# A decoder layer on one core: the second group's first steps moved between the first group's, constants made before zero transfers, PSUM reads ranked first, list transfers yielded in pairs

## The chip, the cores and the metric

The kernel runs on one core of a Trainium2 chip. The metric is the device time of one execution in microseconds (us), lower is better; the median of three runs is given. Engines are named as in the profile: PE (TensorE: matmul, and PEld for its weight loads), DVE (VectorE), ACT (ScalarE), POOL (GpSimd) and SP (SyncE, here a queue that only issues transfers). PSUM is the memory of eight banks that PE writes its results to and DVE and ACT read from.

## What is computed

One decoder layer in f32 on x of 32 batches x 112 tokens x 256, with a context of 375 tokens per batch. Three sublayers, each after a layernorm and each added to x: a delta-rule attention with an MLP, cross attention with 16 heads of 16, and a mixture of 6 experts (two for each token) with one shared expert.

```python
def _L0_attn_ref(x, ...):
    h = _rmsnorm(x, norm1_w)
    q = h @ Wq
    k = h @ Wk
    k = k / jnp.maximum(jnp.linalg.norm(k, axis=-1, keepdims=True), 1e-12)
    v = _ema_scan(h @ Wv, jax.nn.sigmoid(alpha_logit))
    beta = jax.nn.sigmoid(h @ beta_w + beta_b)[..., 0]
    # S += beta_t (v_t - S k_t) k_t^T ;  o_t = S q_t
    attn_out = _delta_scan(q, k, v, beta)
    x = x + attn_out @ Wo
    h2 = _rmsnorm(x, norm2_w)
    return x + (jax.nn.silu(h2 @ w_gate) * (h2 @ w_up)) @ w_down

def _L0_xattn_ref(query, key, value, mask, ...):
    scores = jnp.einsum('bhqd,bhkd->bhqk', Q, K) / np.sqrt(hd)
    scores = jnp.where(mask[:, None, :, :] == 1, -1e9, scores)
    out = jnp.einsum('bhqk,bhkd->bhqd', softmax(scores), V)
    return out.transpose(0, 2, 1, 3).reshape(B, Sq, D) @ w_out.T

def _L0_ffn_ref(x, gate_w, gate_b, ...):
    probs = jax.nn.sigmoid(xt @ gate_w.T + gate_b)
    w, idx = jax.lax.top_k(probs, 2)
    w = w / (jnp.sum(w, axis=-1, keepdims=True) + 1e-08)
    # y = sum over the two experts of w * (silu(x ew1) * (x ew3)) ew2
    return y + (silu(xt @ fc1.T) * (xt @ fc2.T)) @ fc3.T

x = x + _L0_attn_ref(_layernorm(x), ...)
x = x + _L0_xattn_ref(_layernorm(x), ctx, ctx, mask, ...)
x = x + _L0_ffn_ref(_layernorm(x), ...)
```

## The kernel before

**Tiling.** The 32 batches are taken in 8 groups of GB = 4. A group's tile of x is 112 partitions (tokens) x 4 x 256.

**A planner sets the order.** The body doesn't issue instructions; it notes them in a `Recorder` (L76 to L359), which prices each and, in `flush` (L230), schedules them: of the instructions of an engine whose inputs are ready, it takes the one with the lowest `rank` (L227), which is the number of its place in the order of noting. The eight banks are handed out there too. PE, DVE and ACT then run their instructions in that fixed order; POOL's and SP's queues keep theirs, so a transfer that waits holds up those behind it. `flush` is called twice, at the start of the last group and at the end, so the schedule spans groups. All noted instructions have line L358 in the profile (those of the expert tiles L1306 and L1323), so the profile is read by the tiles' names. What stands ahead of the Recorder (L436 to L500: constants, zeroes) is issued directly.

**Generators.** Each piece of a group's work is a generator that yields after every step. `delta_block` (L676) is the first sublayer of a group: `layernorm` (L613) writes a and h, then beta (from hb, the product of h and nwb); `to_features` transposes h to hT and nT; Wk, Wq and Wv projections, the last with a scan (vE); then Gram products G and A, the triangular system W that goes through memory (`blocks`) into blocks L, is solved by DVE for group 0 and by POOL for the others, comes back as X and Y; levels of small products join the blocks (W, Y, X, C); then V, U, oT, x1, h2, and the MLP with gT. `queries` (L917) makes qz. In group 0 nothing else is there to run beside it but the keys and values (kx, vx) of the first batches, which L1429 deals out.

**The main loop** (L1446 to L1532) runs over 128 quads (batch, half and quarter of the heads), 16 per group: `scores` (L966), softmax on DVE and ACT (e, nmx), `turned` (L993, transposes into eT), `product` (L1005, eT by vx), `cross_out` (L1025). Between them it draws steps of three piles: `main`, the first sublayer of the next group (`ahead`), as many as keep its share of the priced work level; `others`, the expert sublayer of the group before (`mixture_sparse`: `route` L1046, `dispatch` L1079, `shared` L1128); and kv, the keys and values of the next batch.

**Experts.** Groups 0 to 6 send their tokens to experts through eight lists in memory: `dispatch` writes the places of the tokens by indirect transfers on POOL; `tables` (L1179) gathers the lists, and `sparse_tiles` runs 54 tiles of 128 tokens (L1306, L1323). The last group runs all experts densely. During the last group's quads `tiles` (tables and the sparse tiles) are drawn after a table of numbers (L1479).

**Buffers.** A `Ring` (L47) hands out buffers of a tag in turn; an instruction that writes a buffer waits for the last reader of what it held. Tag "a", "vo" and "qk" of the delta block have one buffer each, so a second group's a, vE or gT waits for the first group's to be read.

Of the kernel before, what the change touches and what calls it, by code (L numbers as in the profile page):

```python
# [70 lines left out]

class Node:
    __slots__ = ("at", "eng", "cost", "lag", "calls", "before", "after", "banks", "keys", "start", "end", "left", "seen")


class Recorder:  # L76
# [87 lines left out]
    def add(self, name, op, outs, ins, call, cost=None, loose=False):  # L164
# [8 lines left out]
        if not joins:  # L173
            node = Node()
            node.at, node.eng, node.cost, node.lag = len(self.nodes), eng, 0.0, 0.0
            node.calls, node.before, node.after, node.banks, node.keys = [], {}, [], [], set()
            node.start = node.end = None
            node.seen = own if self.whole is None else None
            self.nodes.append(node)
            if self.whole is not None:  # L180
                self.held, node.cost = node, self.whole
# [44 lines left out]

    def rank(self, node):  # L227
        return node.at
# [134 lines left out]
def tile_decoder(ctx: ExitStack, tc: tile.TileContext, t: dict, out: bass.AP):  # L363
# [28 lines left out]
    room = {"mk": SK, "e": 4 * SK, "eT": KC * 4 * T, "qz": 4 * NT, "x": GB * D, "neg": SK, "h": GB * D, "rs_i": 2 * GB, "rs_u": 2 * GB}  # L392
# [68 lines left out]
    for table in lists:  # L461
        nc.gpsimd.dma_start(out=table.rearrange("(p l) o -> p (l o)", p=TM), in_=zeros)
    nothing = moe.tile([P, t["fc3T"].shape[0] // P, NT], F32, tag="hT", name="nothing")
    nothing = nothing[:T].rearrange("p c n -> p (c n)")[:, : NB * FAR // T]
    nc.vector.memset(nothing, 0.0)
    for table in blocks[1:]:
        nc.gpsimd.dma_start(
            out=table.rearrange("n f -> (n f)").rearrange("(p q) -> p q", p=T), in_=nothing
        )
# [29 lines left out]
    for vx in vxs:  # L499
        nc.gpsimd.memset(vx[:, :, :, 1, :], 0.0)  # L500

# [111 lines left out]
    def layernorm(dst, src, rms=None):  # L613
# [15 lines left out]
        for b in range(GB):  # L629
            nc.vector.tensor_scalar(  # L630
                dst[:, b, :], src[:, b, :], mv[:, b, 0:1], r[:, b : b + 1], ALU.subtract, ALU.mult
            )
        if rms is not None:
            off = stat("off")
            nc.vector.scalar_tensor_tensor(off, mv[:, :, 0], -1.0, r[:, GB:], ALU.mult, ALU.mult)
            for b in range(GB):
                nc.scalar.activation(
                    rms[:, b, :], src[:, b, :], AF.Identity, bias=off[:, b : b + 1], scale=r[:, GB + b : GB + b + 1]
                )

# [35 lines left out]
    def delta_block(g, xt):  # L676

        a = dlt.tile([T, GB, D], F32, tag="a", name=f"a_{g}")
# [16 lines left out]
        vE = dlt.tile([P, NC, NT], F32, tag="vo", name=f"vE_{g}")  # L695
# [193 lines left out]
        gT = dlt.tile([P, HID // P, NT], F32, tag="qk", name=f"gT_{g}")  # L889
# [189 lines left out]
    def dispatch(g, a3, place, ge):  # L1079
# [27 lines left out]
        for b in range(GB):  # L1107
            for c in range(2):
                i = g * GB + b
                nc.gpsimd.indirect_dma_start(  # L1110
                    out=lists[2 * b + c][:], out_offset=bass.IndirectOffsetOnAxis(ap=row_i[:, c, i : i + 1], axis=0),
                    in_=number[:, c, i : i + 1], in_offset=None,
                )

# [13 lines left out]
    def shared(g, acc, aT, first=lambda: None):  # L1128
# [6 lines left out]
        for i, _ in enumerate(ffn(g, NE, aT, fc1, fc2, fc3, emit)):  # L1135
            yield
            if i == 0:
                first()
                yield
# [39 lines left out]
    def tables():  # L1179
# [52 lines left out]
        for i, table in enumerate(lists):  # L1232
# [7 lines left out]
            if i % GB == GB - 1:  # L1240
# [186 lines left out]

    early_kv = chained(keys_values(0), keys_values(1))
    for i, _ in enumerate(metered(ahead(0))):  # L1429
        for _ in range({5: 2, 6: 2, 7: 2, 8: 2, 9: 1, 11: 1, 18: 2}.get(i, 0)):  # L1430
            next(early_kv, None)
    drain(early_kv)
# [11 lines left out]
    main, others, out_of, kv = ahead(1), iter(()), iter(()), iter(())  # L1444
    at = 0
    for n in range(len(quads) + 2):  # L1446
# [29 lines left out]
        if last:  # L1476
            mains.append(main)
            side += [others] * ((0, 0, 0, 1, 1, 1, 2, 1, 1, 1, 1, 0, 0, 0, 0, 0)[i] if g < groups else 0)
            side += [tiles] * ((0, 0, 0, 0, 0, 0, 0, 1, 1, 1, 0, 1, 4, 4, 4, 4)[i] if g < groups else 3)  # L1479
        else:  # L1480
# [6 lines left out]
            whole = sum(costs) + (four_out + mixed if g else 0.75 * four_out)  # L1487
# [114 lines left out]
```

## Time and profile before

| | |
|---|---|
| median of three runs | 1462.86 us (1461.95 to 1462.88) |
| the profiled execution's own time | 1463.02 us |
| its span in the profile | 1461.2 us |
| PE busy | 1373.3 us (94%) |
| DVE, ACT, POOL busy | 967.8, 704.8, 319.8 us |
| mean clock granted to PE | 0.976 |

The profile shows one execution. The chain of work that ended last, followed back from the last instruction, is 79% PE, 11% DVE, 6% ACT, 3% issue and 1% POOL. An answer of the timeline gives the start, the length, the engine, the line, the operation and what it writes and reads; in brackets, how long the engine had stood idle and what ended that. A table of windows gives, for a stretch of time, the busy time of each engine and the clock. The stages, by the first and last instructions of each: group 0's first sublayer 0 to 130 us, the steady quads to 1132, the last group's quads with the lists to 1206, expert tiles to 1388, and the last group's dense experts and the stores to the end.

### The profile page before, as it was taken

What the parts mean: (1) busy time and instruction counts of PE and PEld (TensorE: products, weight loads), DVE (VectorE), ACT (ScalarE), POOL (GpSimd) and SP (SyncE); (2) the same over time, 40 slices, a digit from 0 to 9 for tenths busy, and PEclk for the clock granted to TensorE, in tenths of its full rate; (3) what the DMA queues carried; (4) which work ended last, traced back from release to release, by engine and by line L of the source; (5) the groups of instructions that cost most, each with busy time, mean ns of one, the idle gap of its engine ahead of it and who ended that gap; (6) DMA issues with size and microseconds to landing.
All of it is one profiled execution on the core that took longest, in us unless ns stands there. A gap on an engine that the chain in (4) does not pass through costs nothing.

```text
span 1461.2 us, 26685 instructions
## 1 busy us (share of the span) xinstructions
PE 1373.3 (94%) x9716; PEld 929.6 (64%) x9716; DVE 967.8 (66%) x3164; ACT 704.8 (48%) x1946; POOL 319.8 (22%) x492
## 2 busy tenths in 40 slices
PE   4479999999999999999999999999999879999998
PEld 2455766676667666766776677667766556666665
DVE  4547676775777578667866786678657645455577
ACT  2024756654665466546654665566546554322110
POOL 3010310320032003200320032003200324556400
PEclk9679999999999999999999999999999989999999
DMA  8100100101010101010101010101015111222283
GB/s 229 40 1 6 35 16 16 48 17 41 16 48 17 41 16 48 17 41 16 48 16 41 16 49 16 42 16 48 16 29 174 17 47 63 83 80 89 69 231 100
DMA packets 77170, 73.13 MB, mean 50 GB/s; under 512 B 29864, under 2 KB 72808, under 8 KB 77040
## 3 DMA queue, kind: packets, MB, share of 16 engines
q1 hardware_dynamic: 69296, 56.00, 14.0%
q0 software_dynamic: 7744, 15.43, 3.6%
q8 instruction: 77, 1.26, 0.4%
q14 instruction: 53, 0.43, 0.1%
HBM read 51.12 MB, written 20.28 MB: 49 GB/s over the span
## 4 chain that ended last, share of the span: by engine, by line
PE 79%; DVE 11%; ACT 6%; issue 3%; POOL 1%; DMA 0%; ACTq 0%; DVEq 0%; POOLq 0%
PE bank L358 69%; PE bank L1306 6%; PE bank L1323 3%; ACT e L358 3%; ACT h L358 2%; DVE rs_u L358 1%; DVE rs_i L358 1%; ACT eT L358 1%; DVE W L358 1%; DVE br L358 1%; DVE x L358 1%; DVE ms L358 1%; DVE vx L358 1%; DVE above L358 1%; POOL C L358 0%
## 5 line engine op out<-in xcount | busy, mean ns | idle before, releaser
L358 ACT ACTIVATE e<-e,nmx 112x375 f32<-112x375 f32 x512 | 306.2, 601 | 141.7 <-DVE nmx L358 141.4
L358 DVE CUSTOM_DVE_ANT_0 e<-bank,neg,flip 112x375 f32<-112x375 f32 x512 | 281.9, 604 | 47.9 <-PE bank L358 47.4
L358 ACT COPY eT<-bank 125x448 f32<-125x448 f32 x384 | 186.4, 531 | 165.6 <-PE bank L358 149.3
L358 PE MATMUL bank<-ident,e 112*125 112x112 f32 x1536 | 207.1, 279 | 12.3 <-DVE vx L358 6.6
L358 PEld LDWEIGHTS bank<-ident,e 112*125 112x125 f32 x1536 | 188.9, 190 | 46.1 <-issue 13.7
L358 PE MATMUL bank<-kx,qz 32*112 32x375 f32 x1024 | 126.2, 527 | 6.4 <-issue 4.4
L358 PE MATMUL bank<-eT,vx 125*32 125x112 f32 x3072 | 102.8, 264 | 5.0 <-issue 5.0
L358 PEld LDWEIGHTS bank<-eT,vx 125*32 125x32 f32 x3072 | 70.1, 109 | 57.2 <-issue 44.8
L1306 PE MATMUL bank<-ew,xT 128*128 x216 | 102.0, 595 | 1.8 <-ACT e L358 1.2
L358 PE MATMUL bank<-w_xwvT,cT 128*125 128x256 f32 x384 | 102.5, 393 | 0.5
L358 PE MATMUL bank<-cT,w_xwkT 128*128 128x375 f32 x256 | 100.1, 516 | 0.0
L358 DVE SCALAR_TENSOR_TENSOR hs<-hs,bank 128x256 f32<-128x256 f32 x108 | 45.4, 421 | 80.7 <-ACT hs L358 72.0
L358 ACT ACTIVATION_READ_ACCUMULATOR e<-e,nmx 112x1 f32 x512 | 97.2, 190 | 0.0
L358 POOL TENSOR_TENSOR u<-h,nwb 112x1024 f32<-112x1024 f32 x7 | 16.8, 2406 | 306.7 <-issue 306.7
L358 DVE SCALAR_TENSOR_TENSOR qk<-qk,bank 128x448 f32<-128x448 f32 x64 | 39.7, 621 | 64.5 <-ACT qk L358 35.6
L358 ACT ACTIVATE hs<-bank 128x256 f32<-128x256 f32 x54 | 20.7, 383 | 116.3 <-PE bank L1306 107.7
L358 PEld LDWEIGHTS bank<-w_xwvT,cT 128*125 128x125 f32 x384 | 66.6, 188 | 14.1 <-issue 4.1
L358 POOL DMA_INDIRECT lists<-number,row_i x56 | 53.0, 946 | 90.7 <-DVE tn L358 57.0
L358 PEld LDWEIGHTS bank<-cT,w_xwkT 128*128 128x128 f32 x256 | 46.0, 198 | 38.9 <-issue 10.2
L358 PEld LDWEIGHTS bank<-kx,qz 32*112 32x112 f32 x1024 | 42.8, 172 | 42.5 <-issue 18.7
L358 POOL DMA_INDIRECT xg<-rows,take x54 | 52.5, 972 | 71.9 <-PE bank L358 60.6
L358 PE MATMUL bank<-ident,h 112*128 112x112 f32 x256 | 40.9, 280 | 27.4 <-ACT h L358 25.2
(242 smaller groups left out, 2390.8 us busy)
## 6 DMA issues: line engine op xcount, KB each, us to landing
cT<-in_ctxT_dram SPq DMA_DIRECT2D x32, 375.0 KB
mk<-in_mask_dram SPq DMA_DIRECT2D x32, 164.1 KB
x<-in_x_dram SPq DMA_DIRECT2D x7, 448.0 KB
rows<-h SPq DMA_DIRECT2D x7, 448.0 KB
kept<-x SPq DMA_DIRECT2D x7, 448.0 KB
e<-results SPq DMA_DIRECT2D x6, 448.0 KB
eT<-results SPq DMA_DIRECT2D x4, 448.0 KB
out_dram<-x SPq DMA_DIRECT2D x4, 448.0 KB
```

The costliest lines, as they stand in the source:

```text
L358: getattr(getattr(self.nc, name), op)(*[real(a) for a in args], **{k: real(v) for k, v in kwargs.items()})
L1306: rec.nc.tensor.matmul(p.real(), xT[:, c, :], w13[:, bass.ds(at[i] * (NC * 2 * MI) + c * 2 * MI, 2 * MI)], start=(c == 0), stop=(c == NC - 1),
L1323: rec.nc.tensor.matmul(p[:, :D].real(), hT[:, c, :], w2[:, bass.ds(at[i] * (CH * D) + c * D, D)], start=(c == 0), stop=(c == CH - 1),)
```

## The change

1. **Own buffers for group 1.** A new `Ring.at` picks a buffer of a tag by number. Group 1's a takes the third buffer of x, its vE the second of "hT"; group 0's gT takes the second of "qz". So group 1 can start its first sublayer while group 0's is under way, and the load of x of group 2, which needs the third x buffer, waits for the reading of group 1's a.
2. **Group 1's first five steps** (layernorm and beta; transposes of h; Wk; Wq; Wv and scans) are drawn between steps 5 to 9 of group 0, and the main loop counts on from there.
3. **`rank`** takes 120 places off an instruction of DVE or ACT that reads a bank, or that is an activation with an accumulated output.
4. **Constants first.** The transfers of zeros to the lists and blocks are issued on POOL after unit, number, head and the zeroes of vx, not before.
5. **`layernorm`** notes the activations that write h ahead of the DVE operations that write a.
6. **Lists.** `dispatch` yields after each batch's two list transfers, `shared` goes on with `dispatch` in each of its first four steps, `tables` yields after each pair of gathers, and the table of `tiles` is one higher at quad 10 of the last group and one lower at quad 12.

The work on each engine is the same in the two programs; its order differs. POOL's sixteen list transfers of the last stage stand one behind the other in both.

```diff
--- before.py
+++ after.py
@@ -69,8 +69,21 @@
         return ap if dtype == F32 else ap.bitcast(dtype)
+    def at(self, tag, i, shape):
+        n = 1
+        for k in shape[1:]:
+            n *= k
+        key = (tag, i)
+        if key not in self.made:
+            self.made[key] = self.pool.tile([P, self.room[tag]], F32, tag=f"{tag}_{i}", name=f"{tag}_{i}")
+        ap = self.made[key][: shape[0], :n]
+        names = "abcdefgh"[: len(shape) - 1]
+        return ap.rearrange(f"p ({' '.join(names)}) -> p {' '.join(names)}", **dict(zip(names[1:], shape[2:])))
 class Node:
-    __slots__ = ("at", "eng", "cost", "lag", "calls", "before", "after", "banks", "keys", "start", "end", "left", "seen")
+    __slots__ = ("at", "eng", "cost", "lag", "calls", "before", "after", "banks", "keys", "start", "end", "left", "seen", "feeds")
 class Recorder:
@@ -175,6 +188,7 @@
             node.at, node.eng, node.cost, node.lag = len(self.nodes), eng, 0.0, 0.0
             node.calls, node.before, node.after, node.banks, node.keys = [], {}, [], [], set()
             node.start = node.end = None
+            node.feeds = op == "activation" and len(outs) > 1
             node.seen = own if self.whole is None else None
             self.nodes.append(node)
             if self.whole is not None:
@@ -224,8 +238,12 @@
     LATE = 0.15
+    AHEAD = 120
     def rank(self, node):
-        return node.at
+        reads = node.eng in ("DVE", "ACT") and (node.keys or node.feeds)
+        return node.at - self.AHEAD if reads else node.at
     def flush(self, open_banks=()):
@@ -389,7 +407,7 @@
     const = ctx.enter_context(tc.tile_pool(name="const", bufs=1))
-    room = {"mk": SK, "e": 4 * SK, "eT": KC * 4 * T, "qz": 4 * NT, "x": GB * D, "neg": SK, "h": GB * D, "rs_i": 2 * GB, "rs_u": 2 * GB}
+    room = {"mk": SK, "e": 4 * SK, "eT": KC * 4 * T, "qz": 4 * NT, "x": GB * D, "neg": SK, "h": GB * D, "rs_i": 2 * GB, "rs_u": 2 * GB, "hT": t["fc3T"].shape[0] // P * NT}
     io = Ring(ctx.enter_context(tc.tile_pool(name="io", bufs=1)), 2, room)
     tok = Ring(ctx.enter_context(tc.tile_pool(name="tok", bufs=1)), 1, room)
     feat = Ring(ctx.enter_context(tc.tile_pool(name="feat", bufs=1)), 1, room)
@@ -458,15 +476,9 @@
     nc.vector.memset(ones, 1.0)
     zeros = att.tile([TM, NE * NL], F32, tag="neg", name="zeros")
     nc.vector.memset(zeros, 0.0)
-    for table in lists:
-        nc.gpsimd.dma_start(out=table.rearrange("(p l) o -> p (l o)", p=TM), in_=zeros)
-    nothing = moe.tile([P, t["fc3T"].shape[0] // P, NT], F32, tag="hT", name="nothing")
+    nothing = moe.at("hT", 0, [P, t["fc3T"].shape[0] // P, NT])
     nothing = nothing[:T].rearrange("p c n -> p (c n)")[:, : NB * FAR // T]
     nc.vector.memset(nothing, 0.0)
-    for table in blocks[1:]:
-        nc.gpsimd.dma_start(
-            out=table.rearrange("n f -> (n f)").rearrange("(p q) -> p q", p=T), in_=nothing
-        )
     unit = const.tile([NB, BS, BS], F32, tag="unit", name="unit")
     nc.gpsimd.memset(unit, 0.0)
@@ -498,6 +510,12 @@
     vxs = [const.tile([KP, KC, H // 2, 3, HD], F32, tag=f"vx{i}", name=f"vx{i}") for i in range(2)]
     for vx in vxs:
         nc.gpsimd.memset(vx[:, :, :, 1, :], 0.0)
+    for table in blocks[1:]:
+        nc.gpsimd.dma_start(
+            out=table.rearrange("n f -> (n f)").rearrange("(p q) -> p q", p=T), in_=nothing
+        )
+    for table in lists:
+        nc.gpsimd.dma_start(out=table.rearrange("(p l) o -> p (l o)", p=TM), in_=zeros)
     rec = Recorder(tc, nc, [ps.tile([P, 512], F32, tag=f"bank{i}", name=f"bank{i}") for i in range(8)])
@@ -626,10 +644,6 @@
             n = 2 * GB
         r = stat("rstd", 2 * GB)
         rsqrt_of(r[:, :n], both[:, :n])
-        for b in range(GB):
-            nc.vector.tensor_scalar(
-                dst[:, b, :], src[:, b, :], mv[:, b, 0:1], r[:, b : b + 1], ALU.subtract, ALU.mult
-            )
         if rms is not None:
             off = stat("off")
             nc.vector.scalar_tensor_tensor(off, mv[:, :, 0], -1.0, r[:, GB:], ALU.mult, ALU.mult)
@@ -637,6 +651,10 @@
                 nc.scalar.activation(
                     rms[:, b, :], src[:, b, :], AF.Identity, bias=off[:, b : b + 1], scale=r[:, GB + b : GB + b + 1]
                 )
+        for b in range(GB):
+            nc.vector.tensor_scalar(
+                dst[:, b, :], src[:, b, :], mv[:, b, 0:1], r[:, b : b + 1], ALU.subtract, ALU.mult
+            )
     def to_features(src, scale=None):
@@ -675,7 +693,8 @@
     def delta_block(g, xt):
-        a = dlt.tile([T, GB, D], F32, tag="a", name=f"a_{g}")
+        a = io.at("x", 2, [T, GB, D]) if g == 1 else dlt.tile([T, GB, D], F32, tag="a", name=f"a_{g}")
         h = tok.tile([T, GB, D], F32, tag="h", name=f"h_{g}", bufs=3)
         layernorm(a, xt, h)
         plain = nc.vector if g == 0 else nc.gpsimd
@@ -692,7 +711,7 @@
         qk = dlt.tile([P, 2 * NC, NT], F32, tag="qk", name=f"qk_{g}")
         qT, kT = qk[:, :NC], qk[:, NC:]
-        vE = dlt.tile([P, NC, NT], F32, tag="vo", name=f"vE_{g}")
+        vE = moe.at("hT", 1, [P, NC, NT]) if g == 1 else dlt.tile([P, NC, NT], F32, tag="vo", name=f"vE_{g}")
         for m in range(NC):
             pk = bank("pk")
             project(pk[:, :NT], wk, m, hT)
@@ -886,7 +905,8 @@
         yield
         h2T = to_features(h2, n2)
         yield
-        gT = dlt.tile([P, HID // P, NT], F32, tag="qk", name=f"gT_{g}")
+        shape = [P, HID // P, NT]
+        gT = dlt.tile(shape, F32, tag="qk", name=f"gT_{g}") if g else feat.at("qz", 1, shape)
         for m in range(HID // P):
             gated(gT[:, m, :], w_gate, w_up, m, h2T)
             yield
@@ -1111,6 +1131,8 @@
                     out=lists[2 * b + c][:], out_offset=bass.IndirectOffsetOnAxis(ap=row_i[:, c, i : i + 1], axis=0),
                     in_=number[:, c, i : i + 1], in_offset=None,
                 )
+            if b < GB - 1:
+                yield
     def ffn(g, e, aT, w1, w3, w2, emit):
         n = w2.shape[1]
@@ -1134,8 +1156,9 @@
         for i, _ in enumerate(ffn(g, NE, aT, fc1, fc2, fc3, emit)):
             yield
+            if i < GB:
+                first()
             if i == 0:
-                first()
                 yield
     def store(g, acc):
@@ -1237,7 +1260,7 @@
                 in_offset=bass.IndirectOffsetOnAxis(ap=srci, axis=0),
             )
             listed.append(part)
-            if i % GB == GB - 1:
+            if i % 2 == 1:
                 yield
         pt = bank("plist")
         for i, part in enumerate(listed):
@@ -1425,10 +1448,16 @@
         yield from queries(g, x_of[g])
+    FRONT = 5
     early_kv = chained(keys_values(0), keys_values(1))
+    main, at = ahead(1), 0
     for i, _ in enumerate(metered(ahead(0))):
         for _ in range({5: 2, 6: 2, 7: 2, 8: 2, 9: 1, 11: 1, 18: 2}.get(i, 0)):
             next(early_kv, None)
+        if 5 <= i < 5 + FRONT:
+            next(main)
+            at += 1
     drain(early_kv)
     def loads():
@@ -1441,8 +1470,7 @@
     idle = [cost < 0.3 for cost in costs]
     costs = [max(cost, 1.4) for cost in costs]
     four_out, mixed = 4 * 5 * 1.1, 9 * 1.7
-    main, others, out_of, kv = ahead(1), iter(()), iter(()), iter(())
-    at = 0
+    others, out_of, kv = iter(()), iter(()), iter(())
     for n in range(len(quads) + 2):
         g, i = divmod(n, per)
         b, q = divmod(n, each)
@@ -1476,7 +1504,7 @@
         if last:
             mains.append(main)
             side += [others] * ((0, 0, 0, 1, 1, 1, 2, 1, 1, 1, 1, 0, 0, 0, 0, 0)[i] if g < groups else 0)
-            side += [tiles] * ((0, 0, 0, 0, 0, 0, 0, 1, 1, 1, 0, 1, 4, 4, 4, 4)[i] if g < groups else 3)
+            side += [tiles] * ((0, 0, 0, 0, 0, 0, 0, 1, 1, 1, 1, 1, 3, 4, 4, 4)[i] if g < groups else 3)
         else:
             if g > 0 and i in (3, 4, 5, 7, 8, 9, 10, 11, 12):
                 side.append(others)
@@ -1484,7 +1512,7 @@
                 x_of[g + 2] = load_x(g + 2)
                 following = ahead(g + 2)
-            whole = sum(costs) + (four_out + mixed if g else 0.75 * four_out)
+            whole = sum(costs) + four_out + mixed if g else sum(costs[FRONT:]) + 0.75 * four_out
             want = whole * (i + 1) / per - sum(1.1 if x is kv else 1.7 for x in side) - gone
             gone += sum(1.1 if x is kv else 1.7 for x in side)
             while at < len(costs) and len(mains) < 3 and (want > costs[at] / 2 or not mains):
```

## The prediction

> **What bounds the kernel now.** I read the page first, then busy time by stage, then the waits of PE, then the timeline of the places where it waits. The page:
>
> ```profile
> span 1461.2 us, 26685 instructions
> ...
> PE 1373.3 (94%) x9716; PEld 929.6 (64%) x9716; DVE 967.8 (66%) x3164; ACT 704.8 (48%) x1946; POOL 319.8 (22%) x492
> ...
> PEclk9679999999999999999999999999999989999999
> ```
>
> PE (matmuls) sets the time: 87.9 us of 1461.2 idle, and a granted clock under full speed in two places, the second and third slice of 36.5 us, and before the last quarter. Cut into my stages (columns: stretch, length, busy us of PE, PEld, DVE, ACT, POOL with counts, clock, DMA share, GB/s):
>
> ```profile
> 0.00:19.10 19.10, 0.00 (x0) 0.03 (x1) 8.61 (x38) 2.23 (x4) 11.35 (x39) 1.00 0.80 225
> 46.60:61.90 15.30, 0.03 (x1) 0.06 (x1) 10.09 (x44) 0.00 (x0) 1.13 (x1) 0.57 0.24 55
> 61.90:97.50 35.60, 24.61 (x105) 19.57 (x105) 12.56 (x36) 6.00 (x17) 3.86 (x3) 0.64 0.00 0
> 146.00:1132.00 986.00, 965.81 (x7685) 667.20 (x7687) 695.36 (x2338) 572.53 (x1588) 175.77 (x320) 0.99 0.13 35
> 1132.00:1206.00 74.00, 62.25 (x502) 41.92 (x495) 42.79 (x167) 39.13 (x115) 20.09 (x21) 0.88 0.16 33
> ```
>
> The opening loses 19.1 + 15.3 + 11.0 us to idling and more to the clock; the long steady stretch loses 20.2 of 986; the list stage (1132 to 1206) 11.75. What ends PE's waits, whole span (total, times, longest):
>
> ```profile
> PE bank L358 <- ACT h L358: 25.2, 2, 19.1
> PE bank L358 <- DMA X<-blocks: 15.3, 1, 15.3
> PE bank L358 <- issue: 9.4, 6, 3.2
> PE bank L358 <- DVE vx L358: 6.6, 12, 0.6
> PE bank L358 <- ACT eT L358: 4.8, 12, 0.6
> PE bank L358 <- DVE W L358: 4.6, 6, 0.8
> ```
>
> The opening line by line: POOL is busy with the zero transfers before it makes the constants, DVE's first operation waits for one of these, and the layernorm of group 0 stands behind it in DVE's fixed order:
>
> ```profile
> 5.22 3.23 POOL L462 DMA_DIRECT2D lists<-neg  x6
> 8.44 1.09 POOL L467 DMA_DIRECT2D blocks<-hT  x2
> ...
> 10.14 0.36 DVE L485 COPY free<-head 128x6 f32<-128x6 f32 x1 [7.65 <-POOL head L483]
> 10.96 0.47 DVE L358 COPY W<-unit 28x256 f32<-28x256 f32 x1 [0.46 <-POOL unit L473]
> 11.36 0.40 DVE L358 BATCH_NORM_STATS2 bst<-x 112x6 f32<-112x256 f32 x1
> ...
> 16.87 1.38 DVE L358 TENSOR_SCALAR a<-x,bmv,rstd 112x256 f32<-112x256 f32 x4
> 18.36 2.07 ACT L358 ACTIVATE h<-x,off,rstd 112x256 f32<-112x256 f32 x4 [12.29 <-DVE off L358]
> 19.10 2.58 PE L358 MATMUL bank<-ident,h 112*128 112x112 f32 x8 [19.10 <-ACT h L358]
> ```
>
> **The change, part by part.**
>
> *Constants first* (with the rms activations ahead of a). The zero transfers held POOL for 0.76 + 0.59 + 3.23 + 1.09 = 5.67 us; without them unit and head are ready near 4.4 and 5.2. SP keeps eight transfers out, so its issues of 5.68 and 6.18 show the pieces of x, issued first, landed by then: the first statistics can start near 5.7 instead of 11.36, 5.65 us earlier. off no longer waits for a (1.38). So ACT's h starts at 18.36 − 5.65 − 1.38 = 11.3 and PE at 12.1 instead of 19.1. The zeros go out later but are first needed by the blocks transfer at 42.79: hidden. They now compete with the loads of 12 to 33 us (lists 8 × 75 KB, blocks 2 × 198 KB, 1 MB: 4.5 us at the 225 GB/s of the first row); of what they push back, cT and x of group 1 were in by about 30, so nothing waits unless they slip 10 us. The multiply nwb (0.73 at 13.67) stands behind them on POOL and feeds beta, which has slack until 39.1.
>
> *PSUM reads first, opening.* nT on DVE came at 22.94, behind hb (1.23) and the beta reduction (1.22); ahead of these, the first projection starts at 24.00 − 7.0 − 1.7 = 15.3. With its first eight matmuls at half clock, the projections, Gram products and keys of the first two batches, PE runs to about 40.6 without a gap (before, 46.5).
>
> *Group 1's first five steps inside group 0's.* They bring the transposes of h and 24 projection matmuls (Wk, Wq, Wv; 3.17 us for eight: 9.5, and 2.5 more at half clock) into the hole in which PE waited 15.3 us for X<-blocks. But DVE, fixed in order, must do V, the masks, and group 1's statistics, rsqrt and a ahead of the block solve, some of it waiting for POOL's product for beta (2.4). The solve was at 50.63 to 57.46 and X landed at 61.87; I place it at 52.7 to 60.4, and PE's restart at 64.8, 2.9 later. PE idles 5.0 us (40.6 to 45.6) for group 1's h, then 3.1 in the moved matmuls and 4.1 before X. The chain of small products to w_gate (61.9 to 97.5, 11.0 idle) stays, only filled a little with Gram products of group 1, and the first scores come at about 134.5 (129.96).
>
> So the scores start later, but with more done: I count 10.4 us of PE work that stood behind (Wv 1.5, Gram 3.2, transposes 1.0, level products 4.7). The fair sum is PE time lost up to the third output projection, by which both orders have the same PE work done (222 and 221 rows). Before: idle 19.1 + 0.2 + 15.3 + 11.0 + 2.0 = 47.5; half clock 2.8 (19.1 to 24.75), 8.4 (61.9 to 83), 2.8 (94.8 to 100.35) = 14.0; together 61.5. After: idle 12.1 + 0.6 + 5.0 + 3.1 + 4.1 + 11.0 + 0.6 + 3.7 (the ramp of the first quads, as 2.0 + 1.8 before) = 40.2; half clock 13.9; together 54. Gain 7.5. Bounds: 0, if the solve slips 4.5 us more with PE empty behind it, to 13, if group 1's layernorm costs the solve nothing (2.9) and the gap of 5.0 is half filled.
>
> [...]
>
> *Load of x_2 waits for a of group 1* (it holds that buffer). Behind it in SP's queue stand later cT and mk. x_2 is not read before group 1's main stage, so 0; if it blocked SP until 60 us, cT of batch 2 would still be 60 us early.
>
> *PSUM reads first, steady.* From 146 to 1132 PE waits 19.4 us for others: vx 6.6, eT 4.8, W 3.8, nmx 2.0, Y 1.3, e 0.9, all reads of PSUM or fed by one. One of them:
>
> ```profile
> 580.79 1.19 DVE L358 TENSOR_TENSOR above<-above,same 112x144 f32<-112x144 f32 x1
> 582.01 0.30 DVE L358 TENSOR_REDUCE place<-above 112x24 f32<-112x144 f32 x1
> 582.23 0.61 DVE L358 TENSOR_TENSOR W<-bank,br 112x448 f32<-112x448 f32 x1
> ...
> 582.90 1.04 PE L358 MATMUL bank<-W,Y 112*112 112x112 f32 x8 [0.76 <-DVE W L358]
> ...
> 584.43 0.41 DVE L358 COPY vx<-bank 125x256 f32<-125x256 f32 x1
> ```
>
> W and vx stand behind routing operations that nobody awaits; in the changed order they stand between these. The waits on vx and W (10.4) should go mostly, of the others (eT, Y, e: ACT reads in sequence) little. I take 9. Bounds: 19.4 (all gone) to −3 (a quarter of the eT and W waits, added on chains that the reads now delay).
>
> *Lists in pairs, dispatch between batches.* PE loses 11.75 idle and about 4.7 of half clock (0.50 from 1165 to 1182) here, 16.4 in all, while POOL makes sixteen list transfers back to back, 1153.1 to 1173.0, and ACT and DVE stand 7.5 and 14.6 us with no releaser among the engines. In the changed order the sixteen are still back to back on POOL; the yields only shift what PE has beside them. I take 0, bounds −3 to +16.4.
>
> *Last stages* (1206 to the end): PE 246.8 of 255.2; same orders but for a shift of one step in the tiles: 0, bounds ±1.
>
> **Sum**, against the profiled execution (1463.02, of which 1.8 lie outside the span; the median of the runs shown is 1462.86, 0.2 below): 1463.0 − 7.5 − 9 = 1446.5.
>
> **Rivals.**
> (a) *The opening alone.* The waits of 0.2 to 0.8 us may be the schedule's error against real durations and come back elsewhere; for it, eT and Y wait on ACT at 58% busy, in order already. 1463.0 − 7.5 = 1455.5.
> (b) *The list stall goes too.* The engines that stand still have no releaser, but the program's own code comes by transfers (q8, 77 packets, 1.26 MB), and a block of it that is due while POOL's sixteen list transfers run may come late; every engine's count up to that stage changes by some rows, so the block may fall elsewhere. 1446.5 minus most of 16.4: 1433. Against it: POOL's stage is as long. [...]
> (c) *Slower: reads first starve the chains.* A layernorm's rsqrt is 14 small DVE operations of 0.17 us in sequence; a read of the 604 ns kind let in before each makes it 14 × 0.6 = 8.4 us longer. Steady DVE is 70% busy and PE never waits there on h or on rstd, so the chains have slack; were it less than this and a quarter of the 8.4 came through, each of 6.75 group periods of 146 us would lose 2.1, 14.2 in all, with the old waits kept: 1463.0 − 7.5 + 14.2 = 1469.7. It decides from 7.5 / 6.75 = 1.1 us a group.
> (d) *The change doesn't do what it says.* The sixteen transfers stay back to back, the solve moves back by all that PE wins, and the reads bring 2: about 1461.
>
> **Chances.** Forecast 0.50 (1440 to 1452), (a) 0.20, (b) 0.10, (c) 0.13, (d) 0.07. A measurement here tells 0.2% (2.9 us) from no change. Faster 0.50 + 0.20 + 0.10 = 0.80; same 0.07; slower 0.13. The range leaves out (c) and the far end of (b): 1430 to 1461.
>
> **What would show it.** First PE work near 12; the first projection near 15; X<-blocks ending PE's wait near 65, after a shorter idle; first scores near 134; in the steady stretch the waits on vx and W under 4 us in all, eT kept; 11 to 12 us idle in the list stage. Wrong if PE's chain restarts after 70, if waits on h or rstd appear in the steady stretch, or if the list stage idles under 4 or over 16.

## The result, and the profile after

The changed kernel took 1454.42 us (median of 6 runs, 1451.89 to 1460.66) against 1462.87 for the kernel before (6 runs, 1461.95 to 1465.60): a ratio of 0.9948, 95% interval 0.9927 to 0.9970. That is 8.45 us faster where 16.4 were forecast: inside the outer range of 1430 to 1461, but above the 1440 to 1452 of the forecast itself, and 1.1 from rival (a). The profiled execution is the fastest of the six (1451.89, span 1450.2). From its page:

```profile
span 1450.2 us, 26668 instructions
...
PE 1376.5 (95%) x9716; PEld 931.8 (64%) x9716; DVE 964.8 (67%) x3164; ACT 701.0 (48%) x1946; POOL 319.8 (22%) x492
...
PEclk9779999999999999999999999999999989999999
```

Stage by stage (table of windows, columns as before), the time to PE's first work and the steady stretch:

```profile
0.00:12.10 12.10, 0.00 (x0) 0.03 (x1) 8.31 (x37) 2.23 (x4) 10.08 (x36) 1.00 0.58 168
...
150.00:1125.00 975.00, 954.44 (x7628) 660.64 (x7627) 688.53 (x2344) 568.92 (x1589) 164.09 (x286) 0.99 0.13 35
```

and what ended PE's waits over the span:

```profile
PE bank L376 <- ACT h L376: 21.3, 5, 12.1
PE bank L376 <- ACT eT L376: 13.4, 9, 5.7
PE bank L376 <- DMA X<-blocks: 8.1, 6, 5.7
...
PE bank L376 <- DVE vx L376: 2.4, 5, 0.5
...
PE bank L376 <- DVE W L376: 1.7, 2, 1.0
```

The first wait is 7.0 shorter, X<-blocks 7.2, vx 4.2, and W (4.6) is down to 1.7. But eT has grown from 4.8 to 13.4, with single waits of 5.7 and 4.9, and the steady stretch still idles 20.6 us of 975. The timeline of the first of these:

```profile
477.43 0.97 ACT L376 COPY eT<-bank 125x448 f32<-125x448 f32 x2 [1.01 <-PE bank L376]
478.05 1.68 PE L376 MATMUL bank<-nT,w_w_gate 128*128 128x448 f32 x4
...
481.17 0.59 PE L376 MATMUL bank<-eT,vx 125*32 125x112 f32 x16
486.88 0.53 ACT L376 COPY eT<-bank 125x448 f32<-125x448 f32 x1 [8.47 <-remote]
...
487.46 0.60 PE L376 MATMUL bank<-eT,vx 125*32 125x112 f32 x8 [5.70 <-ACT eT L376]
```

ACT's third copy of eT needs transposes that PE had finished at 478.2; the semaphore that says so rises at 486.8, and the signals of two later matmuls (479.7, 481.2) with it. "Remote" means that the profile found nobody who had just finished. This I call a late signal. The clock is at half from 484.6 to 491.4, the last 4 us of it while PE works. The second is at 1050.2 to 1059.3. The group's eight list transfers had gone out before it all, back to back on POOL:

```profile
460.24 0.98 POOL L376 DMA_INDIRECT lists<-number,row_i  x1 [6.42 <-ACT e L376]
...
468.97 0.94 POOL L376 DMA_INDIRECT lists<-number,row_i  x1 [0.30 <-issue]
```

To place gains I use the start of the output projection of a batch (four matmuls of w_xwoT by oTx for each); four batches are one group.

| from the trace (us) | before | after | difference |
|---|---|---|---|
| batch 6 reached | 375.4 | 366.8 | -8.6 |
| three groups without a late signal (10 to 14, 14 to 18, 18 to 22), mean | 144.8 | 141.6 | -3.2 each |
| the two groups with one (6 to 10, 22 to 26) | 145.8, 144.7 | 150.3, 148.7 | +4.5, +4.0 |
| batch 26 to the end | 361.0 | 359.7 | -1.3 |

So the opening brought 8.6. The five steady groups would have brought 16.9 at 141.6 each, and the two groups with a late signal took 15.7 of it back. Some 15 us of that are the waits of 5.7 and 4.9 and the 4 and 5 us in which PE works at half clock behind them.

### The profile page after: what moved, and what is told of

Read it like the earlier page. It is cut to its first block, busy times and chain, and to the rows that moved or that the text cites. A ratio compares the mean times of both kernels' runs of the same rounds, so it can differ in the third digit from the quotient of the medians.

```text
span 1450.2 us, 26668 instructions
## 1 busy us (share of the span) xinstructions
PE 1376.5 (95%) x9716; PEld 931.8 (64%) x9716; DVE 964.8 (67%) x3164; ACT 701.0 (48%) x1946; POOL 319.8 (22%) x492
## 4 chain that ended last, share of the span: by engine, by line
PE 71%; DVE 12%; POOL 4%; ACT 3%; DMA 3%; issue 3%; another core or an unknown queue 2%; DVEq 0%; ACTq 0%; SPq 0%
PE bank L376 61%; PE bank L1329 6%; POOL W L376 3%; PE bank L1346 3%; DVE e L376 2%; ACT e L376 2%; DVE rs_u L376 2%; DMA blocks<-W 2%; DVE x L376 1%; DMA X<-blocks 1%; DVE W L376 1%; ACT eT L376 1%; DVE rs_i L376 1%; DVE vx L376 1%
## 5 line engine op out<-in xcount | busy, mean ns | idle before, releaser
L376 DVE SCALAR_TENSOR_TENSOR qk<-qk,bank 128x448 f32<-128x448 f32 x56 | 34.8, 621 | 78.0 <-ACT qk L376 44.7
L1357 POOL DMA_INDIRECT results<-y,put x54 | 53.2, 985 | 39.1 <-DVE y L376 19.6
```

Of the source, the lines that this page charges most:

```text
L376: getattr(getattr(self.nc, name), op)(*[real(a) for a in args], **{k: real(v) for k, v in kwargs.items()})
L1357: sent = rec.nc.gpsimd.indirect_dma_start(out=results[:], out_offset=bass.IndirectOffsetOnAxis(ap=put[:, i : i + 1], axis=0), in_=y, in_of ...
```

## The experiments

Kernels sent together ran on one chip, beside the kernel before. That read 1446 to 1450 us on some chips and 1463 to 1465 on others; the list stage differs (before: 82.6 us from batch 28 to 30 in the first trace, 65.8 in the trace of before_again; changed kernel 78.6 and 61.2). So I compare ratios, and milestones within traces.

| run | ratio (95%) | batch 6 | groups without a late signal | ACT waits of over 4 us on late signals, batches 6 to 26 |
|---|---|---|---|---|
| rank_only | 0.9855 (0.9839 to 0.9870) | 376.5 | 140.0 to 142.6 | none |
| no_rank | 1.0096 (1.0080 to 1.0112) | 371.6 | 146.5 to 147.4 | 1 (4.8) |
| late_lists | 0.9854 (0.9839 to 0.9870) | 369.7 | 141.1 to 141.4 | none |
| spread_lists | 1.0067 (1.0053 to 1.0081) | 373.0 | 140.9 to 150.8 | none |
| after_again | 0.9894 (0.9879 to 0.9909) | 367.9 | 141.7 to 141.8 | 2 |
| before_again | 0.9996 (0.9985 to 1.0008) | 377.3 | 144.7 to 145.8 | none |
| ln_first_group | 0.9847 (0.9833 to 0.9862) | 370.3 | 140.3 to 141.8 | 1 |
| no_pairs | 0.9887 (0.9869 to 0.9906) | 366.9 | 141.5 to 142.9 | 1 |
| ln_only | 1.0082 (1.0067 to 1.0097) | 373.1 | 145.4 to 148.8 | none |
| no_front | 0.9956 (0.9943 to 0.9970) | 367.4 | 141.5 to 141.7 | 2 |
| after_pad64 | 0.9956 (0.9942 to 0.9969) | 367.4 | 141.4 to 143.2 | 2 |
| lf_pad64 | 0.9918 (0.9904 to 0.9931) | 369.0 | 140.4 to 142.0 | 2 |
| ln_first_2 | 0.9927 (0.9909 to 0.9945) | 369.5 | 140.3 to 140.5 | 2 |
| lf_late | 0.9932 (0.9900 to 0.9964) | 371.0 | 140.3 to 141.6 | 1 (4.9, at 1068) |
| lf_shift | 1.0141 (1.0123 to 1.0160) | 377.3 | none is without | 5 |
| after_pad32 | 0.9913 (0.9886 to 0.9941) | 373.0 | 141.5 to 148.0 | none |
| const_only | 0.9985 (0.9975 to 0.9995) | 372.5 | 144.7 to 146.2 | 1 (4.6) |
| lf_nofront | 0.9818 (0.9805 to 0.9832) | 367.4 | 140.2 to 141.7 | 1 |

**What the ranking is worth.** rank_only adds it to the kernel before, no_rank takes it out of the changed kernel:

```diff
     def rank(self, node):
-        return node.at
+        reads = node.eng in ("DVE", "ACT") and (node.keys or node.feeds)
+        return node.at - self.AHEAD if reads else node.at
```

> The kernel before with the ranking of PSUM reads alone (part 3). The profile after suggests that the ranking shortens a steady group from 144.8 us to 141.4 (six groups: 20 us) and that two late signals in the steady stretch gave 17 of it back. If the ranking alone does this: waits on vx and W nearly gone, steady groups of 141 to 142 us wherever no late signal falls, time 1440 to 1462 depending on how many fall. If the gain belonged to the moved first steps instead, groups stay at 144.8 and the time within 2 us of before.

> The changed kernel without the ranking (AHEAD = 0). If the opening gains 7.5 us by itself, as forecast, and the ranking gives the rest: 1453 to 1456, groups of 144.8 us, first PE work still at 12. If the ranking also made the opening (nT ahead of hb): a first projection 1.5 to 2.5 us later and 1457.

rank_only gains 1.45% alone: groups of 140.4 us (median of five), 4.3 less than before, and next to nothing by batch 6. It is the whole gain of the steady stretch, and more than the changed kernel shows. In two of its groups (530 to 805 us) the list of PE's waits has neither vx nor W, which take 1.8 and 1.5 us in before_again (530 to 815). no_rank missed its expectation: not 1453 but slower than before, with groups of 147. Something else in the change makes each group 2.5 us longer. It also answers the question about the opening: its first projection is at 14.70, as in the changed kernel (14.71), so the ranking didn't bring that forward.

**The same kernels again, and without the pairs.**

> The changed kernel itself, again, since the kernel before read 1446.6 us beside the first four experiments and 1462.9 beside the first comparison. If late signals are what took the gain back and come on some chips more than on others: on a chip where before reads near 1446, this reads 1427 to 1437 with no wait of 8 us in the steady stretch (groups of 141.4 us throughout); on a chip where before reads near 1463, 1450 to 1456 with such waits. If the change itself is worth no more than 8 us: 8 us under before on any chip.

> The kernel before, again, for its trace on the same chip. Theory A (late signals differ by chip): where it reads near 1446, the 16.4 us lost in the list stage are gone from its trace (PE idle in that stage under 3 us), and its steady groups stay at 144.8 us. Rival: the steady groups themselves are shorter on another chip.

> The changed kernel without part 6 (dispatch, shared, tables and the table of tiles as before). The order of PE is the same until the last group's list stage. If the pairs are worth nothing, as forecast: within 2 us of the changed kernel. If they let work in beside the sixteen transfers: 3 to 8 us slower, all of it between 1100 and 1200 us.

On this chip the change gains 1.06% (some 15 us); the two late signals are there too (10.3 and 10.1 us of ACT), so the first expectation's link between chip and late signals fell: what differs by chip is the list stage, for both kernels alike. The two traced pairs differ by 11.0 and 10.9 us, the medians by 8.5 and 14.6; how many late signals the executions without a trace had isn't known. Without the pairs the time is within the noise of it. The traces show why: from batch 26 to the last output projection the pairs save 9.3 us (162.1 against 171.4), and from there to the end they lose 6.2 (178.5 against 172.3).

**The layernorm's order.** ln_first_group keeps the new order for group 0 alone, ln_only puts it alone into the kernel before:

```diff
         rsqrt_of(r[:, :n], both[:, :n])
-        for b in range(GB):
-            nc.vector.tensor_scalar(dst[:, b, :], ...)
         if rms is not None:
...
+        for b in range(GB):
+            nc.vector.tensor_scalar(dst[:, b, :], ...)
```

> The changed kernel with the layernorm's new order (activations of h ahead of a) for group 0 alone. Without the ranking, groups of the changed kernel took 147.3 us against 144.8 before, and with it 141.4 against 140.3 of the ranking alone, so something of the change makes each steady group 1 to 2.5 us longer. If it is the layernorm's order: groups of 140.3 us, 5 to 8 us under the changed kernel. If it is another part (the yields of dispatch, the buffers): groups stay at 141.4 and the time within 2 us of the changed kernel.

> The kernel before with the layernorm's new order alone (activations of h ahead of a, all groups). If this order is what lengthens the steady groups by 2.5 us where the ranking is missing (147.3 against 144.8): groups of 147.3 us, PE waits on vx of 2.5 us in each, time 12 to 17 us over before, less 1.4 at the opening. If the longer groups of the run without ranking came from the moved first steps or the buffers: groups of 144.8 us and a time within 2 us of before.

ln_only is 11.4 us slower than before by medians (1475.45 and 1464.09) and its five groups take 147.5 on the mean (737.5 in all), 2.5 more than before (724.9). The timeline of ln_only shows the place, which comes back in most groups:

```profile
371.74 2.35 POOL L358 TENSOR_TENSOR u<-h,nwb 112x1024 f32<-112x1024 f32 x1 [42.35 <-issue]
371.76 2.35 DVE L358 SCALAR_TENSOR_TENSOR rs_u<-rs_u,both 112x4 f32<-112x4 f32 x1
...
374.94 1.38 DVE L358 TENSOR_SCALAR h<-x,bmv,rstd 112x256 f32<-112x256 f32 x4
...
376.70 0.36 PE L358 MATMUL bank<-ident,e 112*125 112x112 f32 x1 [2.51 <-DVE vx L358]
```

The same two places in the kernel before:

```profile
374.88 0.16 DVE L358 SCALAR_TENSOR_TENSOR rs_u<-rs_u,both 112x4 f32<-112x4 f32 x1
...
377.04 1.56 PE L358 MATMUL bank<-ident,e 112*125 112x112 f32 x12 [0.52 <-DVE vx L358]
```

A DVE operation on 112 x 4 numbers, 0.16 us elsewhere, takes 2.35, as long as POOL's product of h and nwb that started 20 ns before. The activations of h now come earlier, so this product starts while DVE is in the next layernorm's chain of small operations; vx comes later, and PE waits 2.51 us for it instead of 0.52. The traces of before and of ln_first_group show no operation of a layernorm's chain so stretched, the changed kernel one in most groups (2.34 to 2.38 us), which goes with the 1.3 us between its groups and those of ln_first_group on one chip (141.7 and 140.4). In the changed kernel rs_u<-rs_i, a product that reads rs_i for both inputs, takes 2.341 us at 365.48, beside POOL's product of 2.350 that began 27 ns before it, and ends 18 ns after that. A TENSOR_SCALAR with one input is stretched as well: one rs_i<-rs_i takes 0.92 in most groups, beside POOL's W<-G,br of 0.93. A RECIPROCAL with one input (br<-ss, 0.18) and operations that read a bank (rank<-bank,free, 0.16) keep their length beside POOL's products.

**The moved first steps and the constants.**

```diff
-    FRONT = 5
+    FRONT = 0
```

> The changed kernel with no step of group 1 drawn into group 0 (FRONT = 0); constants first, the ranking, the layernorm's order and the pairs stay. The forecast gave the opening 7.5 us in all, of which PE's earlier start of 7.0 and the nT order were the larger part of the gain and the moved steps moved the chain 2.9 back but carried 10.4 us of PE work forward. If that working holds: the first scores come some 9 us earlier than in the changed kernel, and group 1 pays it back; time 3 to 8 us over the changed kernel. If the moved steps are worth nothing: within 2 us of it.

> The kernel before with the constants alone made first (transfers of zeros last). The working of the forecast: unit and head ready 5.67 us earlier, so first work of PE at 13.4 in place of 19.1 and the whole opening 5 to 6 us earlier, with the stages behind it as before: 1457 to 1459 where before reads 1463 or 1464 (0.996). If the opening is bound elsewhere (loads, the block solve): within 2 us of before.

no_front reaches batch 6 at 367.4 us and takes 1456.84; after_pad64, the changed kernel with 64 idle matmuls at its start and the same chip, 367.4 and 1456.97. Without the moved steps the first output projection comes 19 us earlier (149.5 against 168.4), and group 1 pays all of it back. Over the whole they are worth nothing. const_only (zero transfers moved behind the zeroes of vx) starts PE at 13.37 as expected, but only 0.15% is left of it. Its timeline:

```profile
15.03 0.74 POOL L358 TENSOR_TENSOR nwb<-nwb,h 112x256 f32<-112x256 f32 x1
15.80 1.23 DVE L358 TENSOR_TENSOR u<-h,nwb 112x1024 f32<-112x1024 f32 x1 [3.21 <-POOL nwb L358]
...
17.88 2.84 PE L358 MATMUL bank<-cT,w_xwkT 128*128 128x375 f32 x4 [1.92 <-DMA w_xwkT<-in_xwkT_dram]
...
18.20 0.68 DVE L358 TENSOR_SCALAR nT<-bank,v_norm_w 128x448 f32<-128x448 f32 x1
...
20.50 4.00 PE L358 MATMUL bank<-nT,w_Wk 128*128 128x448 f32 x8
```

nwb now stands behind the zero transfers on POOL, and DVE idles 3.2 before u (1.1 of it after ACT's last h, which u needs too). nT, which the first projection needs, stands behind u and the beta reduction as before, and PE does keys first, for whose weights it waits 1.92. So the projection starts 7.1 after PE's first work (before: 4.9), and of the 5.7 us gained 3.5 are left there.

What puts nT ahead of u is the layernorm's order and not the ranking: ln_only and no_rank, both without the ranking, start the first projection 2.6 after PE's first work (17.91 and 20.52; 12.09 and 14.70). In rank_only nT is ahead of the beta reduction, but still behind u, and it takes 3.3 (19.33 and 22.64). Constants alone reach batch 6 at 372.5, the layernorm's order alone at 373.1, the ranking alone at 376.5, and all three at 367; before reads 375.4 and 377.3. These traces come from different chips, so whether the parts only add up or help each other isn't shown.

**What makes the signals late.** late_lists holds the list transfers of groups 0 to 5 until group 5's routing, spread_lists ties each pair to a later quad; the pads add small matmuls at the start.

```diff
+        if g == groups - 3:
+            z = stat("z", 1)
+            nc.vector.tensor_scalar(z, rank[:, 0, 0:1], 0.0, None, ALU.mult)
+            nc.vector.tensor_scalar(row_f[:, :, : g * GB], row_f[:, :, : g * GB], z, None, ALU.add)
+            two = slice(0, (g + 1) * GB)
+        if g >= groups - 3:
+            nc.vector.tensor_copy(row_i[:, :, two], row_f[:, :, two])
...
+    for _ in range(64):
+        nc.tensor.matmul(banks[0][:32, :1], ident[:, :32], ident[:, :1], start=True, stop=True)
```

> The changed kernel, but the list transfers of groups 0 to 5 all wait for group 5's routing (a product with zero of its ranks is added to their places), so no list transfer runs before some 1030 us and 48 run from there on. Theory A (POOL's list transfers make PE's signals late some 8 us after them): no wait of ACT on a late signal of 8 us before 1030, all five groups before it 141.4 us long, the milestone at 1000 us some 8 us earlier than in the changed kernel; time 1437 to 1448, more if the 60 us of transfers near 1030 make signals late many times. Theory B (the late signals come from the loading of PE's code, whose blocks fall where they fell): a wait of 8 us near 480 stays, and the time stays within 3 us of 1454.

> The changed kernel, but each pair of list transfers of a steady group waits for the softmax of a later quad (a product with zero is added to its places), so pairs come some 9 us apart instead of eight back to back. If it is the run of eight in 10 us that makes signals late: no such wait in the steady stretch, 1437 to 1442 us and a narrow spread over the runs. If any list transfer can do it: waits of 8 us as often or more often than before the edit, 1450 to 1460.

> The changed kernel with 64 small matmuls more at the very start, while PE waits for its first input (each with its weight load: 128 instructions, half a code block of 16 KB; PE takes a block in some 17.6 us, so every later block is asked for some 8.8 us earlier). Nothing else moves. If the late signals hang on a code block of PE that is asked for a few microseconds behind the list transfers: the wait of 8 to 10 us near 480 us is gone or has moved to another group, and the time is 1427 to 1436 where before reads 1450. If they hang on the list transfers alone, whatever PE loads: the wait near 480 stays, and the time stays near 0.989 of before.

> The same 64 matmuls ahead of the kernel with the layernorm's new order for group 0 alone, which had one such wait (480 us, 7 us of PE and half clock after it). By the block theory: no wait there and 1414 to 1420 where before reads 1450, the fastest so far, unless another group catches one. By the rival: 1427 as without the matmuls.

late_lists fits theory A: no late signal and groups of 141.1 to 141.4, on the chip on which no_rank had one. But rank_only, on the same chip and with the transfers in place, has none either; a cleaner pair follows. spread_lists has no late signal, but its added dependencies cost PE waits of 2.6 to 4.8 us on the MLP's output in three of five groups, so its time settles nothing. The pads failed as a test: an f32 matmul here is two instructions, each with its weight load, so 64 of them are 256 (after_pad64's timeline has 128 matmuls for them), about one whole code block (252 on the mean: 77 packets of 16 KB on q8 for 19432 matmuls and weight loads in the changed kernel), and each block was asked for when it had been before (475.7 against 475.5 us). The late signals stayed. The next four repair that; the first three have the same order on PE until the last group:

> The kernel with the layernorm's new order for group 0 alone, again, as the measure for the next two: 0.985 to 0.992 of before, with a wait of ACT of 8 to 10 us on a late signal near 480 us.

> The same, with the list transfers of groups 0 to 5 held until group 5's routing (as late_lists). PE's order is the same up to the last group. If the transfers make the signals late: no such wait before 1030 us, every group 140.4 us, no code block that takes over 2 us to load before 1030, and 6 to 12 us under ln_first_2, less what the 48 transfers cost near 1110 (5 us in late_lists). If PE's code blocks alone do: the wait near 480 stays.

> The same, with each group's eight transfers held back by three quads (some 27 us), back to back as before. If it takes both, transfers and a code block asked for 4 to 7 us behind them: the wait near 480 goes, and others may come in other groups, 25 to 40 us behind where the transfers stood. If the transfers alone do, whatever is loaded: a wait in the second group, now near 507. If the code alone: still near 480.

> The changed kernel with 32 small f32 matmuls at the start, which come out as 128 instructions: half a block of PE's code, so that each block is asked for some 8 us earlier than in the changed kernel (near 467 in place of 475.5). If a code block asked for just behind the transfers is needed: no wait near 480, perhaps one in another group. If the transfers alone do: the wait near 480 stays.

ACT's waits on late signals for eT (total, times, longest), first in the changed kernel between 150 and 1125 us, then in lf_shift between 150 and 1130:

```profile
ACT eT L376 <- remote: 17.6, 2, 9.1
```

```profile
ACT eT L376 <- remote: 58.3, 6, 9.8
```

lf_late has none before 1020 us, where ln_first_2 has one. In lf_shift, which holds each group's eight transfers back by three quads, all six groups have one, and it stands in the transfers themselves:

```profile
350.64 0.54 ACT L376 ACTIVATE qk<-bank 128x448 f32<-128x448 f32 x1 [0.35 <-PE bank L376]
360.95 0.53 ACT L376 COPY eT<-bank 125x448 f32<-125x448 f32 x1 [9.76 <-remote]
```

POOL issues its eight from 349.5 to 359.3. PE's signals rise at 355.2, 356.6, 358.0, 359.4 and 360.9, one in 1.4 us, about the pace of the transfers (1.24). So in these traces the late signals go with the transfers, wherever these stand: none before 1020 us with the transfers held back, six with them moved. They are not enough: before batch 26 they run in every group of before and rank_only without such a wait of ACT, and in three of the changed kernel's five.

What else it takes is open. Code blocks were the suspect. Blocks of PE's code take about 1 us to load (median 0.98 to 1.09, by trace), but longer beside the transfers: of 92 blocks asked for between a run's first transfer and 10 us behind its last (all traces, 150 to 1025 us), 76 took 2 to 4 us, of 980 others two did. The wait near 480 follows such a block (475.5, 2.99 us), and between 470 and 490 the trace has hardly any other transfer (32 small packets). But four other groups of the same trace had such a block (2.9 to 3.5 us) and no late signal that PE waited for; the second late signal, from 1050.2, has no block of PE between 1033.7 and 1061.1; and in lf_shift five of the six waits have no slow block of PE in them. after_pad32, half a block of code, has none in the steady stretch, as if PE's code phase mattered, but this is one trace, and not the shift that was meant: its transfers ran later too (470.5 in place of 460.2), and the block was asked for at 476.0, not 467.

Neither cure pays as it is. lf_late is no faster than ln_first_2 (0.9932 against 0.9927) and its runs spread from 1446.6 to 1461.2: beside the 48 transfers signals are late near 1068 (4.9 us) and 1082 and in the list stage. after_pad32 lost 2.8 us at 430 us and 2.3 at 1005 to X<-blocks, in groups of 148.0 and 146.2. lf_shift is 33 us slower than ln_first_2.

**The fastest.** lf_nofront has ranking, constants first and pairs, the layernorm's order for group 0 alone and no moved steps:

> The changed kernel without the moved first steps and with the layernorm's new order for group 0 alone (ranking, constants first and pairs stay). If the moved steps are worth nothing and the layernorm's order costs 1.1 us a group, as the runs so far say: the time of the kernel with both groups' steps and that order (0.985 to 0.993 of before by chip), within 3 us. If the moved steps help once the order is mended: 3 to 9 us slower than that.

1421.76 us against 1447.75: 0.9818. By this ratio it beats the changed kernel too (0.9894 at best, on another chip), with one late signal left (477.2 to 485.8).

## Why the prediction was wrong, and where it was right

**The opening** came out line by line: PE at 12.10 (12.1), first projection 14.71 (15.3), X<-blocks releasing PE at 63.55 (64.8), w_gate 101.78 (97.5 before, put some 3 later), first scores 134.56 (134.5). Up to the third output projection, where 7.5 were summed, the trace is 7.9 earlier (232.9 and 225.0), and by batch 6 8.6. The total hid two wrong parts. The moved steps were credited with carrying 10.4 us of PE work forward, against a chain 2.9 later. They move it 10.9 later (X<-blocks at 52.70 in no_front), are 2.5 ahead at the third output projection (225.3 in after_pad64, 227.8 in no_front) and nothing at the fourth (263.0, 263.1). And the 1.7 us by which nT moves ahead were given to the ranking; no_rank has them without it, from the layernorm's order.

**PSUM reads first, steady** was mis-sized: 9 us forecast for the stretch, 4.3 a group measured (rank_only), 21 us over five groups, beyond the upper bound of 19.4, which stood for nearly seven. The term took the listed waits and halved them. Over two groups, PE's idle time fell from 7.1 to 4.0 us (before_again and after_again, from batch 10 to 18), half clock of 3.4 us went, and 64 transposes of h went from 9.8 to 6.4 us, counted from start to start: waits too short for the list. The ranking also takes small operations out from beside POOL: ms<-r takes 1.19 in before_again and 0.16 in rank_only. How much of the 4.3 that is was not measured apart.

**The step that failed outright** is "rms activations ahead of a": it was given its 1.38 us at the opening and no cost in the other groups. It costs 2.5 us a group alone (ln_only), 1.3 under the ranking, because POOL's product then runs beside DVE's chain. The trace of before had the warning: ms<-r at 1.2 to 1.5 us instead of 0.16 wherever POOL's x<-x,u ran beside it.

**The term that was missing** are the late signals: the list transfers were weighed in the last stage only (0, and right there: 1.3 us from batch 26 to the end), though the same eight run in every group. Rival (b) named the list transfers, in another place, and code blocks, for which the late signals don't speak. Against the 16.5 us that were summed, the profiled pair has 1.1 more at the opening, 7.9 more in five steady groups (16.9 at 141.6 us each, with the layernorm's cost in it), 1.3 at the end, and 15.7 less in the two groups with a late signal: 11.1. The median run is another 2.5 us slower than the profiled one. That the time still fell into the outer range is luck: a steady gain nearly twice as large as forecast and a loss that was not forecast pull against each other. None of the three signs of being wrong appeared (X<-blocks at 63.55, no wait on h or rstd in the steady stretch, 10.1 us idle from 1125 to 1200): they didn't cover what failed. Rivals (a) and (c) gave times near the measured one (1455.5) or beyond it, but not for their reasons: the steady waits did go, and no chain starved.

## What to carry to other kernels

Read the small operations of a chain for outliers before moving work: an operation of 0.16 us that takes 2.35 names the engine whose work it must not run beside, and an edit that brings that work forward has a price in every later group. Measure each part alone and the sum without it: here the part with the most code was worth nothing and the short ranking most of it (0.9855 alone, 0.9818 for the fastest kernel, on two chips). A gain that is missing from the total can sit in a few long waits with no releaser: list them, and look what else ran in the 20 us before.

## What the runs showed of the hardware

- A DVE operation with two inputs took as long as a POOL product that began 20 to 33 ns before it: 2.35 us in place of 0.16 (rs_u<-rs_u,both at 371.76 in ln_only; rs_u<-rs_i in five groups of the changed kernel, 2.34 to 2.38, ending 15 to 20 ns after the product). A TENSOR_SCALAR with one input took 0.92 beside a product of 0.93, in place of 0.17. A RECIPROCAL kept its 0.18 and operations that read a bank their 0.16; so did rs_u<-rs_i at 415.45 in the changed kernel, 0.16 beside a small W<-W of 0.34 that began 4 ns before.
- With runs of eight indirect transfers on POOL, PE's semaphores rose late in places: 8.6 us after the matmul's end at 478.2 and 8.5 after that at 1050.7 in the changed kernel, 11.5 after that at 477.0 in no_pairs. The two matmuls of the changed kernel ended 9.3 and 8.0 us behind the issue of the last transfer (468.97, 1042.77). In lf_shift, while the transfers ran, the signals rose one in 1.4 us. With the transfers held back (late_lists and lf_late) ACT had no such wait from 150 to 1020 us. Of 92 blocks of code asked for beside the transfers 76 took 2 to 4 us to load; the median of all blocks is 0.98 to 1.09, by trace.
- Chips differ by 17 us in this kernel's list stage alone, 82.6 against 65.8 us for the same two batches.
- The granted clock fell and returned in steps: all stretches at half clock in the changed kernel's trace, but for the last at its end, are 3.4, 6.8, 17.1 or 23.9 us long, multiples of 3.41. The one of 6.8 from 44.27 follows a gap of 4.15 us in PE's work that ended at 43.39.
